# A planned attention-and-recurrence kernel: a shift of rank for each part of the work, and measured lengths for bunches of small matmuls

## The chip, the cores and the metric

The kernel runs on one core of a Trainium2 chip, in float32 throughout. The core has five engines with a queue of instructions each: TensorE (PE) for matmuls, VectorE (DVE), ScalarE (ACT), GpSimd (POOL), and SyncE (SP), which issues the transfers (DMAs). Each engine works through its own queue in order; engines wait for each other by semaphores. The metric is device time in microseconds, lower is better. The kernel before takes 1836.63 us (median of three runs, 1832.29 to 1839.57).

## The reference, cut to what matters

There are 32 batches. Each has two matrices of 128 x 512. A cross attention comes first, then one block of a recurrent layer with 32 heads of size 16 over a sequence of 128 steps.

```python
# attention, for each batch: x_c = x, x_s = ctx
Mn = Wn @ inorm(x_c) + bn;  Mm = Wm @ inorm(x_s) + bm
A  = softmax(Mn.T @ Mm, axis=-1)                   # 512 x 512
x  = Wo @ ((Wl @ x_s + bl) @ A.T) + bo + x_c
# recurrent block, 128 steps, 512 channels
xa = ln(x); sx = shift(xa) - xa                    # shift: the step before
xxx = tanh((xa + sx * maa_x) @ maa_w1)             # five mixes
xk, xw, xv, xr, xg = (xa + sx * (maa_j + xxx_j @ maa_w2_j) for j in "kwvrg")
w = exp(-exp(time_decay + tanh(xw @ td_w1) @ td_w2))
r, k, v, g = xr @ Wr.T, xk @ Wk.T, xv @ Wv.T, silu(xg @ Wg.T)
for t in range(128):                               # for each head: state s, 16 x 16
    a = outer(k[t], v[t]);  out[t] = r[t] @ (u * a + s);  s = a + w[t][:, None] * s
x1 = x + (groupnorm(out) * g) @ Wo.T
xc = ln(x1); xk2, xr2 = two more mixes of xc with its shift
return x1 + sigmoid(xr2 @ Wfr.T) * (square(relu(xk2 @ Wfk.T)) @ Wfv.T)
```

## The kernel before, in words

The 32 batches form eight groups of four (`G = 4`, `NG = 8`), so a tile holds 128 channels by 4 x 128 steps: 128 x 512. `layer0(b)` is the attention of one batch: four matmuls of scores (128 x 512 each), a maximum on DVE, an exponential on ACT, the division on DVE, sixteen transposes on PE with copies on ACT, and four matmuls with the values. `layer1(g)` is the recurrent block of a group. Its parts follow each other: the front (normalisation, shift, low-rank matmuls), the mixes (DVE, then POOL adds), gates, two halves of the recurrence (`c = 0` and `c = 2`, two tiles of channels each), the head (group norm, `Wo`), and `feed_forward` (norm, squares, rows, and the store of the result).

The recurrence has no loop over steps. Scores between steps are made level by level, for blocks of 1, 2, 4, 8, 16 and 32 steps: after each level DVE multiplies r and k by decays (`twice`), ACT spreads r over two tiles (`wide`), and a *bunch* of 64 small matmuls (32 rows each) makes the scores, which DVE copies under a mask (`level`), or ACT plainly for the last level, into `at`. When all levels are done, the scaled k is transposed (8 transposes in a bunch), copied by ACT, and three kinds of bunches follow: the state in mid-sequence (32 matmuls, `ps`), the outputs from the state (64, `po`), and twice 64 matmuls that add `at` times v.

The kernel's code does not fix the order of instructions. `Program.record` keeps every operation, and `Program.run` (line 225 on) asks `schedule` for an order and emits it; so all instructions bear line L234. `schedule` is a planner: it estimates each operation's length (`cost`; a bunch's is written by hand in `K.bunch(ns)`), and `order_of` walks through time and takes, among the operations that can start soonest on an engine, the one with the lowest rank. The rank is the operation's place in the written order, less a small share of the length of the chain behind it. In sixteen rounds the planner lowers the ranks of what came before PE's longest gaps, and keeps the best order by its own reckoning. It also decides which buffer each tensor gets: 8 banks of PSUM, 44 work tiles (`t`), and four places for weights of 1 MB (`wring`). The attention of the next group's batches is written in among the parts of the present group (`ahead`), so that PE has other work during the recurrence. The last two groups overlap in another way: the feed-forward of group 6 runs within group 7 (`later`, `place`).

SP issues all large transfers in the order that the planner gives. Four weights pass through each of the four `wring` places in turn; `Wg`, `Wk` and `Wr` for a group are loaded while the group before ends, when its `Wo`, `Wfk`, `Wfr` and `Wfv` leave their places. The stores of the result (`out_dram`, four per group) go through the same queue, after a POOL addition each.

Of the kernel before, what the change touches and what calls it, by code (L numbers as in the profile page):

```python
# [23 lines left out]
G = 4  # L24
NG = B // G
# [34 lines left out]
LAG = 130  # L60
SWITCH = 95
ROUNDS, TRACE, BLAME = 16, 20000, 0.001
REACH, PULL = 200, 0.003
WORDS, REFILL = 280, 3200
TABLE = {AF.Exp: ("exp",), AF.Tanh: ("exp", "sigmoid"), AF.Sigmoid: ("sigmoid",), AF.Sqrt: ("sqrt",)}
# [230 lines left out]
    return ns, ns  # L296


def schedule(ops):


    for op in ops:
        for b in op.before:
            b.after.append(op)


    chain = [0.0] * len(ops)
    for op in reversed(ops):
        i = op.index
        chain[i] = op.ns + max(  # L310
            [chain[a.index] + LAG for a in op.after if a.index < i + REACH], default=0.0
        )
        op.rank = i - PULL * chain[i]
    best = None
    for turn in range(ROUNDS):
        order = order_of(ops)
        end = max(op.end for op in ops)
        if best is None or end < best[0]:
            best = end, order, [(t, t.slot) for op in ops for t in op.first], [op.rank for op in ops]
            since = 0  # L320
        else:
            since += 1
        if since == 4:

            for op, rank in zip(ops, best[3]):
                op.rank = rank
            since = 0
        free = 0.0
        for op in order:
            if op.engine != "PE":  # L330
                continue
            gap, free = op.start - free, op.end
            if gap < 200:
                continue
            late = op
            while late and late.end > op.start - TRACE:
                late.rank -= BLAME * min(gap, 3000) * (1 + turn % 4)
                late = max(late.before, key=lambda b: b.end, default=None)
    for t, slot in best[2]:
        t.slot = slot  # L340
    return best[1]
# [203 lines left out]
def xattn_then_rwkv(ctx: ExitStack, tc: tile.TileContext, a: dict, out: bass.AP):  # L545
# [74 lines left out]
        return vec[:, i, c : c + 1]  # L620

    def constants():
        K.stage = ("constants",)

        def load(t, src):
            K.held = begun[0]
            K.sync.dma_start(t, src)

        load(vec, a["vec"])
        rows = wt([2 * B, E])  # L630
        for r in range(2):
            load(rows[r * B : (r + 1) * B, :], a["ctx_2048"][:, r, :])
        load(w1, a["maa_w1"].rearrange("(c p) m -> p c m", p=P))
        load(w2a, a["maa_w2"][0:P, :])
        for c in range(NC):
            load(w2b[c * DM : (c + 1) * DM, :], a["maa_w2"][P : P + DM, c * P : (c + 1) * P])
        load(td1, a["td_w1"].rearrange("(c p) m -> p c m", p=P))
        for i in range(2):
            load(td2[i * DD : (i + 1) * DD, :], a["td_w2"])
        load(wv, a["WvT"].rearrange("(c p) o -> p c o", p=P))  # L640


        pt = bank()
        for c in range(NC):
            K.tensor.transpose(
                pt[:, c * 2 * B : (c + 1) * 2 * B], rows[:, c * P : (c + 1) * P],
                ident[0 : 2 * B, 0 : 2 * B],
            )
        K.vector.tensor_copy(st.rearrange("p c r b -> p (c r b)"), pt[:, 0 : NC * 2 * B])

        def block_ones(t, pattern, first, step, width):

            K.gpsimd.memset(t, 1.0)
            K.gpsimd.affine_select(
                out=t, in_=t, compare_op=ALU.is_ge, fill=0.0, base=first,
                pattern=pattern, channel_multiplier=step,
            )
            K.gpsimd.affine_select(
                out=t, in_=t, compare_op=ALU.is_ge, fill=0.0, base=width - 1 - first,
                pattern=[[-s, n] for s, n in pattern], channel_multiplier=-step,  # L660
            )


        for n in (DM, DD):
            part = st_(n)
            K.vector.tensor_reduce(part, ident.rearrange("p (i m) -> p m i", m=n), AX.X, ALU.add)
            K.vector.tensor_copy(
                fold[n].rearrange("p (i m) -> p i m", m=n),
                part.unsqueeze(1).to_broadcast([P, P // n, n]),
            )  # L670

        block_ones(heads, [[-S, DM]], 0, 1, S)

        K.vector.tensor_copy(sum_bc, heads[:, 0:H8].unsqueeze(2).to_broadcast([P, H8, S]))

        K.vector.tensor_reduce(
            par, heads[:, 0:H8].rearrange("p (q x) -> p x q", x=2), AX.X, ALU.add
        )

        K.vector.tensor_scalar(heads, heads, 1.0 / S, None, ALU.mult)  # L680


        for l in level:
            flt = st_(C // 2)
            for n in range(2):
                block_ones(flt[n * C : (n + 1) * C, :], [[-2 * l, C // 2 // l], [0, l]], 0, 1, l)
            K.vector.tensor_copy(level[l], flt)

        for c in range(NC):
            block_ones(heads_t[c * DM : c * DM + H8, :], [[1, P]], 0, -S, S)  # L690


        wvh = wv.rearrange("p c (h j) -> p (c h) j", j=S)
        wvm = wt([P, NC * NH])
        K.vector.tensor_reduce(wvm, wvh, AX.X, ALU.add)
        K.vector.tensor_scalar(wvm, wvm, 1.0 / S, None, ALU.mult)
        K.vector.tensor_tensor(
            wvh, wvh, wvm.unsqueeze(2).to_broadcast([P, NC * NH, S]), ALU.subtract
        )
# [17 lines left out]


    def layer0(b):
        K.stage = ("first", b)  # L720
        x_c, x_s = wt(), wt()
        K.held = begun.get(b - 2)
        K.sync.dma_start(x_c, a["x"][b])
# [114 lines left out]
    def recurrence(c, ex, xk, xr, xv, wk, wr, s0m):  # L838
# [5 lines left out]
        for i in range(2):  # L844
            K.scalar.copy(r[i], proj(wr, xr, c + i))
            K.scalar.copy(k[i], proj(wk, xk, c + i))
            K.scalar.copy(v[i], proj(wv, xv, c + i))

# [48 lines left out]
        for i in range(2):  # L900
# [14 lines left out]
            for s in range(2):  # L915
                K.vector.tensor_tensor(right, right, t2.view(s, (4, nb), (2, 2)), ALU.add)

        for l in LEVELS:


# [6 lines left out]
                    AF.Identity, scale=par[:, x : x + 1],  # L927
                )
            pa = [bank() for _ in range(Q4)]
            with K.bunch(2 * 843):  # L930
                for i in range(2):
                    for b in range(G):
                        for n in range(2):
                            for q in range(Q4):
                                rows_q = slice(q * DM, (q + 1) * DM)
                                at_ = i * N + b * L + n * C
                                K.tensor.matmul(
                                    pa[q][n * C : (n + 1) * C, (i * G + b) * C : (i * G + b + 1) * C],
                                    rk[rows_q].view(2 * N + at_, (1, C)),
                                    r2[rows_q, (i * G + b) * 2 + n],  # L940
                                    start=True, stop=True,
                                )
# [31 lines left out]
            kt.append(wt([C, N]))  # L974
            K.scalar.copy(kt[i], pk[i][0:C, :])
        ps = bank()
        with K.bunch(2 * 385):
            for i in range(2):
                for b in range(G):
                    for q in range(Q4):  # L980
                        at_ = i * VP + (b * Q4 + q) * 2 * DM
                        K.tensor.matmul(
                            ps[q * DM : (q + 1) * DM, (i * G + b) * DM : (i * G + b + 1) * DM],
                            kt[i][:, b * P + q * DM : b * P + (q + 1) * DM],
                            vp[0:C].view(at_, (DM + S, 2), (1, S)),
                            start=True, stop=True,
                        )
        s1 = wt([P, 2 * G, 2 * S])
        for x in range(2):
# [3 lines left out]
                ALU.mult, ALU.add,  # L993
            )


        po = [bank() for _ in range(2)]
        with K.bunch(2 * 1020):
            for i in range(2):
                for b in range(G):  # L1000
                    for n in range(2):
# [7 lines left out]
                                start=(i == 0 and b == 0), stop=False, skip_group_check=True,  # L1009
                            )  # L1010
        for i in range(2):
            with K.bunch(2 * 760):
                for b in range(G):
                    for x in range(2):
                        for n in range(2):
# [18 lines left out]
    def layer1(g, xs):  # L1034
# [14 lines left out]
                    if p == i:  # L1049
                        next(later[0])  # L1050

        K.stage = ("front", g)
        s0 = wt([P, G, NC, S])
        for i in range(G):
            K.held = begun[g * G + 1]
# [46 lines left out]
        low_g = wt()  # L1102
        K.scalar.activation(low_g, pl, AF.Tanh)


        xm = {n: [] for n in "kwvrg"}
        pg = [bank() for _ in range(NC)]
# [41 lines left out]
        dlow = wt()  # L1149
        K.scalar.activation(dlow, pd, AF.Tanh)  # L1150

        gates = []
        for c in range(NC):
            pg = proj(wg, xm["g"], c)
# [4 lines left out]

        o = []  # L1160
        for c in range(0, NC, 2):
            K.stage = ("recurrence", g, c)
            if g == NG - 1 and c == 2:
                last_ws[:] = [weight(n, holds) for n in ("Wfk", "Wfr")]
            holds = K.ops[-1]
            place(c // 2)
            K.stage = ("recurrence", g, c)
            ex = decays(c, dlow)
            K.stage = ("recurrence", g, c)
            if c == 2:  # L1170
                third = K.ops[-1]
            ahead(c)
            o += recurrence(c, ex, xm["k"], xm["r"], xm["v"], wk, wr, s0m)
            ahead(c + 1)
        K.stage = ("back", g)
        wo = weight("Wo", third)
        if g == NG - 1:
            last_ws.append(weight("Wfv", third))
# [1 line left out]
            ws = [weight(n, third) for n in ("Wfk", "Wfr", "Wfv")]  # L1180

        place(2)
        K.stage = ("back", g)

        pvar = bank()
        sq = []
# [44 lines left out]

    def feed_forward(g, xs, ws):

        K.stage = ("back", g)
        xc, sx2 = norm_shift(xs, "ln2_w", "ln2_b", 0, g)
        xk2, xr2 = [], []
        for c in range(NC):
# [6 lines left out]
            )  # L1244
            xr2.append(sx2[c])
        yield
        K.stage = ("back", g)
        kk = []
        for eo in range(NC):
            pk = proj(ws[0], xk2, eo)  # L1250
# [2 lines left out]
            K.vector.tensor_tensor(t, t, pk, ALU.mult)  # L1253
            kk.append(t)
        yield
        K.stage = ("back", g)
        wfr, wfv = ws[1:]
        for i in range(G):
            sl = slice(i * L, (i + 1) * L)
# [64 lines left out]
```

## Time and profile before

| what | us |
|---|---|
| median of three runs | 1836.63 |
| the profiled execution's own time | 1835.13 |
| its span, first to last instruction | 1833.4 |
| PE busy | 1775.9 (97%) |
| DVE busy | 1170.1 (64%) |
| ACT busy | 704.2 (38%) |
| POOL busy | 310.0 (17%) |
| one matmul pass of 128 x 512, start to start (a matmul takes two) | 0.43 |
| a bunch of level scores, shortest | 1.52 |
| 1 MB of weights, issue to landing | 5.0 to 6.8 |

In a row of the timeline stand the start, the length of the merged instructions, the engine, line, operation, tiles (written<-read), shape, how many records, and in brackets the idle time of the engine ahead of it with what ended it. A float32 matmul leaves two records, a transpose one; so a bunch of 64 matmuls has 128. PEclk is the share of PE's clock that was granted. "issue" as a reason means that the profile shows nothing that the engine waited for.

### The profile page before, as it was taken

Reading aid. Unit: us, or ns where it says so; the run is one execution under the profiler, and the core shown is the slowest. Engines: PE = TensorE matmul, PEld = TensorE weight load, DVE = VectorE, ACT = ScalarE, POOL = GpSimd, SP = SyncE. Lnnn points to the kernel's source line nnn. Section 1 sums busy time; section 2 is a strip of 40 time slices with the busy share of each in tenths; the row PEclk is TensorE's granted clock in tenths of the full one; section 3 lists DMA queues with packets and bytes.
Section 4 is the critical chain, followed back from the end, with each engine's and each line's share of the span. In section 5 each row is a group of like instructions: output and inputs, shape, how many; then the busy total and the mean of one; then the engine's idle time right before and its main releaser. Section 6 shows DMA issues by size and latency. Waiting matters only on the chain. (4 is left out here: it accounts for less than half of the span.)

```text
span 1833.4 us, 45471 instructions
## 1 busy us (share of the span) xinstructions
PE 1775.9 (97%) x20232; PEld 885.6 (48%) x20232; DVE 1170.1 (64%) x2301; ACT 704.2 (38%) x1230; POOL 310.0 (17%) x329
## 2 busy tenths in 40 slices
PE   8999999999999999999999999999999999999998
PEld 4445543455434554345543455434554345545543
DVE  9748783398634886448764487645876466756652
ACT  5334531445313553235532354323543254324421
POOL 2320006000060001600016000160000600410011
PEclk9999999999999999999999999999999999899999
DMA  6002112020121101221011110112101121002000
GB/s 208 23 23 63 26 54 73 23 71 19 58 69 46 52 14 58 69 70 29 14 63 65 69 30 14 63 63 70 30 13 64 41 60 49 3 24 71 4 18 29
DMA packets 61939, 87.22 MB, mean 48 GB/s; under 512 B 20336, under 2 KB 21488, under 8 KB 61744
## 3 DMA queue, kind: packets, MB, share of 16 engines
q1 hardware_dynamic: 61024, 84.06, 14.2%
q8 instruction: 158, 2.59, 0.6%
q14 instruction: 37, 0.30, 0.1%
q10 hardware_dynamic: 720, 0.26, 0.1%
HBM read 75.93 MB, written 8.39 MB: 46 GB/s over the span
## 5 line engine op out<-in xcount | busy, mean ns | idle before, releaser
L234 PE MATMUL bank<-t,wring 128*128 128x512 f32 x1024 | 473.4, 599 | 3.4 <-DVE t L234 3.3
L234 PE MATMUL bank<-wring,t 128*128 128x512 f32 x768 | 342.5, 597 | 0.0
L234 DVE TENSOR_TENSOR t<-bank,t 128x512 f32<-128x512 f32 (+1 forms) x256 | 143.8, 585 | 265.5 <-PE bank L234 182.0
L234 PEld LDWEIGHTS bank<-t,wring 128*128 128x128 f32 x1024 | 184.4, 190 | 238.4 <-issue 209.0
L234 POOL TENSOR_TENSOR t<-t,t 128x512 f32<-128x512 f32 x192 | 239.9, 1287 | 312.0 <-DVE t L234 311.3
L234 POOL TENSOR_TENSOR small<-small,neg_half 128x1 f32<-128x1 f32 (+1 forms) x96 | 62.5, 663 | 1206.1 <-DVE small L234 1196.9
L234 PE MATMUL bank<-t,t 128*128 128x512 f32 x512 | 255.1, 609 | 0.2 <-ACT t L234 0.2
L234 PEld LDWEIGHTS bank<-wring,t 128*128 128x128 f32 x768 | 143.9, 191 | 189.9 <-issue 179.8
L234 ACT COPY t<-bank 128x512 f32<-128x512 f32 (+1 forms) x240 | 132.2, 588 | 228.7 <-PE bank L234 222.0
L234 ACT ACTIVATE t<-bank 128x512 f32<-128x512 f32 x120 | 71.5, 597 | 367.7 <-PE bank L234 283.1
L234 DVE SCALAR_TENSOR_TENSOR t<-bank,vec,t 128x512 f32<-128x512 f32 x192 | 134.3, 745 | 60.1 <-PE bank L234 49.9
L234 PEld LDWEIGHTS bank<-ident,t 128*128 128x128 f32 x900 | 106.9, 140 | 95.5 <-issue 61.7
L234 PE MATMUL bank<-ident,t 128*128 128x128 f32 x900 | 141.2, 277 | 3.5 <-ACT at L234 2.4
L234 ACT ACTIVATE wide<-rk,par 128x512 f32<-128x512 f32 x128 | 85.4, 715 | 127.2 <-DVE rk L234 127.0
L234 PE MATMUL bank<-t,wv 128*128 128x512 f32 x256 | 123.8, 598 | 0.2
L234 PEld LDWEIGHTS bank<-wide,rk 32*64 32x64 f32 x8192 | 96.9, 131 | 55.9 <-issue 27.1
L234 PEld LDWEIGHTS bank<-t,t 128*128 128x128 f32 x512 | 85.4, 189 | 79.0 <-issue 52.4
L234 DVE COPY_PREDICATED at<-level,bank 128x512 f32<-128x512 int32 x192 | 123.1, 706 | 0.0
L234 ACT ACTIVATE t<-bank,small 128x512 f32<-128x512 f32 x128 | 87.6, 688 | 89.6 <-DVE small L234 88.1
L234 PE MATMUL bank<-wide,rk 32*64 32x64 f32 x8192 | 108.0, 233 | 7.9 <-issue 5.2
L234 DVE TENSOR_REDUCE small<-bank 128x1 f32<-128x512 f32 x128 | 85.4, 685 | 38.2 <-PE bank L234 37.9
L234 DVE TENSOR_SCALAR t<-t,small,small 128x512 f32<-128x512 f32 x128 | 67.4, 546 | 39.9 <-POOL small L234 36.8
(98 smaller groups left out, 1815.7 us busy)
## 6 DMA issues: line engine op xcount, KB each, us to landing
t<-in_ctx_dram SPq DMA_DIRECT2D x32, 256.0 KB, 3.0
t<-in_x_dram SPq DMA_DIRECT2D x32, 256.0 KB, 3.0
wring<-in_WgT_dram SPq DMA_DIRECT2D x8, 1024.0 KB, 5.5
wring<-in_WkT_dram SPq DMA_DIRECT2D x8, 1024.0 KB, 5.1
wring<-in_WrT_dram SPq DMA_DIRECT2D x8, 1024.0 KB, 5.3
wring<-in_WoT_dram SPq DMA_DIRECT2D x8, 1024.0 KB, 5.5
out_dram<-t SPq DMA_DIRECT2D x32, 256.0 KB, 2.0
wring<-in_WfkT_dram SPq DMA_DIRECT2D x7, 1024.0 KB, 5.0
```

What stands on the lines that cost most here:

```text
L234: f(*[real(x) for x in args], **{k: real(x) for k, x in kw.items()})
```

## The change

Each recorded operation already carried the name of its part (`K.stage`). The change gives the stages finer names and all of them the same form (kind, group or batch, half), adds a table of shifts in rank by stage, and adds an operation's shift to its rank; a key with "+" holds for the last groups in addition (the last four batches for "first", the last two groups for others). The shifts were found by random trials of the planner. Besides, four lengths of bunches are set to values measured on the chip. Nothing else is changed: no operation, no buffer count.

```diff
+SHIFTS = {
+    "first0": -306, "first0+": -95, "first1": 2, "first1+": -122, "first2": -40,
+    "first2+": -7, "first3": 24, "first3+": 203, "front": 7, "front+": 157, "gates": -67,
+    "gates+": -1, "head": -121, "head+": 51, "levels0": -68, "levels0+": -71, "levels2": 20,
+    "levels2+": -152, "mixes": 81, "mixes+": -41, "norm": 78, "norm+": -310,
+    "outputs0": -277, "outputs0+": 238, "outputs2": -235, "outputs2+": -661,
+    "recurrence0": -14, "recurrence0+": -48, "recurrence2+": -68, "rows": 85, "rows+": 306,
+    "squares": -88, "squares+": 77, "values0": -56, "values0+": -63, "values2": 33,
+    "values2+": 81,
+}
...
+def shift(op):
+    kind, of, sub = op.stage
+    last = of >= (NG - 1) * G if kind == "first" else of >= NG - 2
+    return SHIFTS.get(kind + sub, 0) + (SHIFTS.get(kind + sub + "+", 0) if last else 0)
...
-        op.rank = i - PULL * chain[i]
+        op.rank = i - PULL * chain[i] + shift(op)
...
-            with K.bunch(2 * 843):        # level scores
+            with K.bunch(1522):
...
-        with K.bunch(2 * 385):            # state in mid-sequence
+        with K.bunch(686):
...
-        with K.bunch(2 * 1020):           # outputs from the state
+        with K.bunch(1920):
...
-            with K.bunch(2 * 760):        # at times v
+            with K.bunch(1412):
```

The new stage names: "first" with the batch's place in its group, "recurrence" split into "recurrence", "values", "levels" and "outputs" (each with its half, 0 or 2), "front" split into "front", "mixes" and "gates", and "back" into "head", "norm", "squares" and "rows".

More of the change, by code (lines that the diff above doesn't have):

```diff
@@ L622, in constants @@
     def constants():
-        K.stage = ("constants",)
+        K.stage = ("constants", 0, "")
         def load(t, src):
@@ L719, in layer0 @@
     def layer0(b):
-        K.stage = ("first", b)
+        K.stage = ("first", b, str(b % G))
         x_c, x_s = wt(), wt()
@@ L847, in recurrence @@
             K.scalar.copy(v[i], proj(wv, xv, c + i))
+        K.stage = ("values", K.stage[1], K.stage[2])
         VP = G * Q4 * 2 * DM
@@ L916, in recurrence @@
                 K.vector.tensor_tensor(right, right, t2.view(s, (4, nb), (2, 2)), ALU.add)
+        K.stage = ("levels", K.stage[1], K.stage[2])
         for l in LEVELS:
@@ L994, in recurrence @@
             )
+        K.stage = ("outputs", K.stage[1], K.stage[2])
         po = [bank() for _ in range(2)]
-        with K.bunch(2 * 1020):
+        with K.bunch(1920):
             for i in range(2):
@@ L1050, in place @@
                         next(later[0])
-        K.stage = ("front", g)
+        K.stage = ("front", g, "")
         s0 = wt([P, G, NC, S])
@@ L1103, in layer1 @@
         K.scalar.activation(low_g, pl, AF.Tanh)
+        K.stage = ("mixes", g, "")
         xm = {n: [] for n in "kwvrg"}
@@ L1150, in layer1 @@
         K.scalar.activation(dlow, pd, AF.Tanh)
+        K.stage = ("gates", g, "")
         gates = []
@@ L1161, in layer1 @@
         for c in range(0, NC, 2):
-            K.stage = ("recurrence", g, c)
+            K.stage = ("recurrence", g, str(c))
             if g == NG - 1 and c == 2:
@@ L1166, in layer1 @@
             place(c // 2)
-            K.stage = ("recurrence", g, c)
+            K.stage = ("recurrence", g, str(c))
             ex = decays(c, dlow)
-            K.stage = ("recurrence", g, c)
+            K.stage = ("recurrence", g, str(c))
             if c == 2:
@@ L1174, in layer1 @@
             ahead(c + 1)
-        K.stage = ("back", g)
+        K.stage = ("head", g, "")
         wo = weight("Wo", third)
@@ L1182, in layer1 @@
         place(2)
-        K.stage = ("back", g)
+        K.stage = ("head", g, "")
         pvar = bank()
@@ L1232, in feed_forward @@
     def feed_forward(g, xs, ws):
-        K.stage = ("back", g)
+        K.stage = ("norm", g, "")
         xc, sx2 = norm_shift(xs, "ln2_w", "ln2_b", 0, g)
@@ L1246, in feed_forward @@
         yield
-        K.stage = ("back", g)
+        K.stage = ("squares", g, "")
         kk = []
@@ L1255, in feed_forward @@
         yield
-        K.stage = ("back", g)
+        K.stage = ("rows", g, "")
         wfr, wfv = ws[1:]
```

## The prediction

> **What bounds the kernel now.** I read the page first:
>
> ```profile
> span 1833.4 us, 45471 instructions
> PE 1775.9 (97%) x20232; PEld 885.6 (48%) x20232; DVE 1170.1 (64%) x2301; ACT 704.2 (38%) x1230; POOL 310.0 (17%) x329
> PEclk9999999999999999999999999999999999899999
> ```
>
> TensorE (PE) is the bound: it is idle for 1833.4 - 1775.9 = 57.5 us. Of these, 6.3 pass before its first matmul (the chain of waits names the DMA of WoT) and 5.1 after its last, which ends at 1828.3. So 46.1 us are left to an order, and besides them what is hidden inside "busy": bunches of small matmuls that run long, and time at half clock. Next, busy time by stretch (the columns after the stretch: its length, then PE, weight loads, DVE, ACT, POOL, PE clock, DMA):
>
> ```profile
> 604.00:690.00 86.00, 81.47 (x1909) 48.72 (x1897) 70.58 (x142) 45.89 (x88) 3.75 (x6) 1.00 0.09 23
> 690.00:829.00 139.00, 138.38 (x632) 60.53 (x635) 73.59 (x144) 42.31 (x66) 33.54 (x30) 1.00 0.19 65
> 829.00:915.00 86.00, 80.75 (x1909) 48.42 (x1901) 70.79 (x142) 45.91 (x88) 3.75 (x6) 0.98 0.09 23
> 915.00:1057.00 142.00, 141.39 (x648) 61.87 (x649) 73.67 (x144) 42.30 (x66) 33.55 (x30) 1.00 0.18 63
> 454.48:457.89 3.41, 3.41 (x4) 1.34 (x5) 3.41 (x6) 0.69 (x1) 0.00 (x0) 0.50 0.00 0
> 1580.88:1591.12 10.24, 9.07 (x176) 5.09 (x165) 9.83 (x14) 3.39 (x6) 9.39 (x7) 0.50 0.01 2
> 680.00:683.41 3.41, 2.46 (x5) 0.97 (x6) 3.41 (x6) 1.13 (x2) 0.00 (x0) 1.00 0.00 0
> ```
>
> A group takes about 226 us, and its idle sits in one part: 4.5 and 5.3 us in the 86 us from mid-recurrence to the head, 0.6 in the 140 us between. The five such parts of groups 1 to 5 sum to 24.3 us, 0 to 240 us holds 9.5 after the first matmul, and 1546 to 1612 us 4.4. The timeline of PE in group 3, and two places of group 2 that recur in each group, say what ends the waits:
>
> ```profile
> 839.07 1.59 PE L234 MATMUL bank<-wide,rk 32*64 32x64 f32 x128
> 842.13 1.06 PE L234 MATMUL bank<-ident,rk 128*64 128x128 f32 x8 [1.47 <-DVE rk L234]
> 844.62 0.76 PE L234 MATMUL bank<-vp,t 64*32 64x32 f32 x64 [0.57 <-ACT t L234]
> ...
> 858.07 1.12 PE L234 MATMUL bank<-wide,rk 32*64 32x64 f32 x80
> 859.89 0.77 PE L234 MATMUL bank<-wide,rk 32*64 32x64 f32 x48 [0.70 <-issue]
> 860.59 1.12 PE L234 MATMUL bank<-t,t 128*128 128x512 f32 x2
> ```
> ```profile
> 680.95 1.12 PE L234 MATMUL bank<-t,WnT 128*128 128x512 f32 x2 [1.11 <-DVE t L234]
> 706.75 2.81 PE L234 MATMUL bank<-t,wring 128*128 128x512 f32 x6 [0.58 <-DVE t L234]
> ```
>
> PE has run out of other ready work there; its DVE or ACT partner then sets the end.
>
> **The change part by part.** It adds and removes no instruction: matmuls, ACT table loads (46) and 194 transfers are the same. All of it is the order, read from the built programs. I lay PE's instructions out at their undisturbed traced durations and ask, for each wait, how much PE work stands between the instruction that starts a chain and the one that needs its result.
>
> *Bunch lengths.* 1686 becomes 1522 ns for a bunch of level scores, others likewise. The chip's bunch costs what it did (the one at 1568.54 is followed at 1570.06): 0 us by itself. Only the planner's idea of what covers a chain gets truer.
>
> *Groups 1 to 5, the 86 us part.* (1) Between the last level bunch and the transposes of k stood nothing; the need is 842.13 - 839.07 - 1.52 = 1.54 us. Now two projection matmuls of 0.86 us and two changes of tile shape stand there, 1.81 us: saves 1.54. (2) Transposes to the state bunch: need 1.62, cover 0.95, now 3.52: saves 0.63. (3) The next half's first level bunch came 1.6 us after the previous bunch and took 860.59 - 858.07 = 2.52 instead of 1.52; now 11.7 us lie between: saves 1.00. (4) State bunch to output bunch in the second half: 0.85 us apart, with stretches of 0.28 and 0.66; now 2.0. Bunches 1.9 apart still stretch by 0 to 0.77, so half: 0.5. (5) Transposes of the softmax at 880 us waiting for DVE: 0.38. (6) The bank held by the head's product (680.95): 1.27 with the restart. (7) 706.75: 0.75. For 5 to 7 no chain of the new order lacks over 0.06 us of cover. Sum 6.07 per group. Against it: this ignores queues on DVE, busy 70.6 of 86 us. In the order before, chains alone explain about 3.4 of the 4.6 us of waits, so queues added 1.2; I leave 1.2 in: 4.87 x 5 = 24.4 us. Ends: 12 (half comes back) and 30 (none).
>
> At (3) the Trainium skill speaks against me: "Runtime: NRT & Kernel Launch", Instruction fetch mechanics, says that code is fetched in 16 KiB blocks of 256 instructions and that crossing into the next is mostly hidden. A bunch has 128 matmul and 128 weight-load records, one block. By the rule, spacing is worth 0 and 3 and 4 fall away (-7.5 us); the row shows 1.00 us at one bunch. I go by the row.
>
> *Group 0.* The first phase of batch 4 moves ahead of group 0's front (places 102 to 169 of PE's 2740 planned operations, before 136 to 189). POOL's twenty adds of 1.29 us for the mixes are then later: about 4 us more wait near 90 us. Later the order has the covers of (1) and (2), where waits of 1.8, 0.9, 0.7 and three of 0.5 stood, and stretches that sum to 2.8: about 8. Net 4, ends 0 and 8.
>
> *From group 6 to 7 (1546 to 1612 us).* Four level bunches stand close; the new order leaves 0.53 us between the third and fourth and 0 before the transposes: 3.2 + 1.6 us uncovered, against 4.4 idle before. POOL's adds for the last mixes lack about 9 us of cover, where they lacked 14. Gain 2, ends -4 and +6. Group 7's output bunches go from 0.95 to 1.8 us apart: gain 1, ends 0 and 2.
>
> *Half clock.* At 454 and 908 us the clock halves for 3.41 us after wait (6): 2 x 1.7 us. "TensorE: Matmul & The Clock Gate", What's actually happening, asks for an idle window of about 3.4 us; the row has 1.11 us of idle, and at 680 us the same wait left the clock at 1.00. By the rule closing (6) brings 0 here, by the row up to 3.4: I take 2. The rule also warns that the 3.2 us hole at group 6 to 7 may halve the clock again; so of the 10.24 + 6.83 us at half clock there (8.5 us) I count nothing as won.
>
> *Shapes and DMA.* Changes of tile shape fall from 461 to 456, 0.09 us each: 0.5. SP issues in order, and WrT stands behind three output stores; before, it was issued at 750.75 and used at 757.46, 6.7 us for a load of about 5.3:
>
> ```profile
> 750.75 0.39 SPq L234 DMA_DIRECT2D wring<-in_WrT_dram  x1
> ```
>
> Now the PE work between the slot's release and the use is 0.8 us shorter: 5.9 us, still enough; I charge 0.5, up to 3.
>
> Sum: 24.4 + 4 + 2 + 1 + 2 + 0.5 - 0.5 = 33.4 us. The profiled execution took 1835.1 (1833.4 span and 1.7 around it): 1801.7. The median of the runs is 1836.6, 1.5 above; I give **1803 us**.
>
> **The rivals.** *Queues take half back.* DVE is busy 82% of the 86 us part; the chains get cover but arrive behind others. For it: 1.2 us per group already. Against: the idle is at few places. Half of 33: 1819 us.
>
> *No change.* The trials fitted the planner, which knows nothing of half clock and guesses the fetch of code; PE then waits at new places. Against: the uncovered places of 3.4 us per group are gone in the order itself. 1836 us, within 0.5%, which is about what a measurement of this kernel can tell.
>
> *Slower: POOL holds up WrT.* The third store waits for POOL's third output add. One mix add stood ahead of that add in POOL's row of outputs and mixes; now eight do (10 us). By durations the store is ready 2.4 us before WrT's slot (3.3 before), and WrT has 0.6 us to spare. If the add comes over 3.0 us later than that, PE stops at the projection, each further us costing 1 us in five groups. From 3.0 + 33.4 / 5 = 9.7 us on the kernel is slower; at 13 us it ends at 1853. Against: POOL has 4.2 of 16.9 us free there.
>
> **How the numbers follow.** Likeliest 62%, own range 1790 to 1815: the ends of the parts, not all at once. Queues 22%, 1815 to 1827. No change 9%. Slower 7%. The bound of 0.5% lies at 1827.4, so faster is 0.84, same 0.09, slower 0.07. The range of 8 in 10 runs from 1788 to 1828.
>
> **What would show it.** In the 86 us parts PE idle falls from about 5 to 1 to 2 us; the 1.47 wait for rk and the 1.11 before WnT are gone; the first level bunch of the second half takes 1.5 us; no half clock near 454 and 908 us; near 1500 to 1600 us waits and half clock stay. I am wrong if PE's waits for DVE in groups 1 to 5 keep their sum, if a wait for WrT appears, or if PE's busy time grows by what its idle loses.

## The result, and the profile after

The changed kernel takes 1808.97 us (median; 1808.35 to 1811.91) beside 1834.46 (1829.71 to 1839.57) for the kernel before on the same chip: a ratio of 0.9864, 95% interval 0.9833 to 0.9895, or 25.5 us less. Beside the other experiments it gave 1808.25 and 0.9872 (0.9857 to 0.9886). Forecast were 1803 us, with 1788 to 1828 as the range: the sign and the range were right. The time is 6 us above the forecast; of the forecast gain of 33.4 us, 8 are missing (the kernel before, measured again, took 2 us less than in the forecast). How the 25.5 us came about is not how the forecast summed them.

The head of the page after, as the prediction showed it of before:

```profile
span 1807.2 us, 45445 instructions
PE 1761.2 (97%) x20232; PEld 889.7 (49%) x20232; DVE 1170.0 (65%) x2301; ACT 706.0 (39%) x1230; POOL 310.0 (17%) x329
```

PE's idle time is 1807.2 - 1761.2 = 46.0 us (57.5 before), and its busy time is 14.7 us less for the same 20232 matmuls: part of the gain was hidden in "busy". What PE waited for, first the kernel before, then the changed one (in total, times, longest, all in us):

```profile
PE bank L234 <- issue: 13.4, 28, 1.4
PE bank L234 <- DVE t L234: 12.2, 16, 1.1
PE bank L234 <- DVE rk L234: 7.3, 5, 1.5
PE bank L234 <- ACT t L234: 4.9, 8, 1.6
```
```profile
PE bank L244 <- issue: 17.4, 20, 2.4
PE bank L244 <- DVE t L244: 6.6, 7, 1.8
PE bank L244 <- ACT t L244: 4.9, 10, 1.8
PE bank L244 <- DVE rk L244: 1.4, 1, 1.4
```

The waits for DVE have shrunk, as forecast: those for rk from five to one. But "issue", time in which PE waited for nothing that the profile shows, has grown from 13.4 to 17.4 us, and its longest from 1.4 to 2.4. Busy time by stretch (columns: the stretch, its length, PE, weight loads, DVE, ACT, POOL, PE clock, DMA share, GB/s):

```profile
458.00:595.00 137.00, 136.71 (x892) 62.76 (x891) 82.04 (x160) 43.61 (x68) 34.84 (x32) 1.00 0.14 47
595.00:681.00 86.00, 82.49 (x1642) 48.01 (x1641) 62.03 (x129) 44.97 (x86) 2.89 (x4) 1.00 0.18 53
815.00:901.00 86.00, 84.58 (x1716) 49.54 (x1705) 64.27 (x135) 47.22 (x89) 2.89 (x4) 1.00 0.18 53
384.16:387.57 3.41, 3.41 (x36) 1.98 (x36) 1.09 (x1) 1.33 (x2) 0.00 (x0) 0.50 0.87 204
97.44:104.26 6.82, 6.82 (x11) 2.84 (x10) 3.77 (x6) 0.00 (x0) 6.82 (x7) 0.50 0.01 2
```

The five 86 us parts now hold 1.4 to 4.2 us of idle, 3.0, 3.5, 1.4, 2.8 and 4.2 in groups 1 to 5, where the prediction said 1 to 2. The half clock of 454 and 908 us is gone; there is a new one at 97 us, 6.8 us long, and in this execution one at 384.

To see more than idle I took each piece of PE work (a planned operation) from its start to the next one's start, against the undisturbed time of the same kind of work. What is over is excess, and I sorted it: waits for other engines; half clock; excess of the bunches of 32 or more small matmuls that is no such wait ("code"); and the rest. Each number is one execution's. In us, before then after:

| part of the kernel | waits | half clock | code | rest |
|---|---|---|---|---|
| group 0 | 6.4, 3.4 | 0, 3.4 | 3.7, 3.5 | 10.4, 9.2 |
| groups 1 to 5 | 20.0, 3.2 | 3.4, 1.7 | 13.0, 16.7 | 25.8, 19.1 |
| to the passage from 6 to 7 | 0.9, 1.0 | 0, 0 | 1.3, 0.2 | 3.6, 2.6 |
| passage | 4.3, 6.7 | 8.2, 4.4 | 0.9, 1.0 | 2.0, 2.2 |
| end | 0.4, 2.5 | 0, 0 | 5.6, 1.9 | 2.4, 3.2 |
| all | 32.0, 16.7 | 11.6, 9.5 | 24.5, 23.4 | 44.3, 36.2 |

In groups 1 to 5 the waits fell by 16.8 us. The "code" excess, of which the prediction took 7.5 us away, rose by 3.7. Here is where it sits: PE's timeline in group 2 of the changed kernel, from the last level bunch of the first half to its second output bunch, then the first level bunch of the second half, and SP's queue.

```profile
592.36 1.59 PE L244 MATMUL bank<-wide,rk 32*64 32x64 f32 x128
593.88 1.98 PE L244 MATMUL bank<-t,wring 128*128 128x512 f32 x4
595.70 1.05 PE L244 MATMUL bank<-ident,rk 128*64 128x128 f32 x8
...
600.11 0.76 PE L244 MATMUL bank<-vp,t 64*32 64x32 f32 x64
600.80 1.13 PE L244 MATMUL bank<-t,wring 128*128 128x512 f32 x2
601.76 1.02 PE L244 MATMUL bank<-t,wv 128*128 128x512 f32 x2
602.72 1.87 PE L244 MATMUL bank<-rk,t 32*32 32x64 f32 x119
606.46 0.35 PE L244 MATMUL bank<-rk,t 32*32 32x64 f32 x9 [1.87 <-issue]
...
608.65 1.37 PE L244 MATMUL bank<-at,vp 64*32 64x64 f32 x115
611.01 0.34 PE L244 MATMUL bank<-at,vp 64*32 64x64 f32 x13 [0.99 <-issue]
...
626.91 1.59 PE L244 MATMUL bank<-wide,rk 32*64 32x64 f32 x128
```
```profile
599.36 0.37 SPq L244 DMA_DIRECT2D wring<-in_WfrT_dram  x1
601.96 0.37 SPq L244 DMA_DIRECT2D wring<-in_WfvT_dram  x1
```

The transposes of k (595.70) follow two projection matmuls and wait for nothing; that is step (1) as forecast. The projections of the second half, PE's cover, now run to 601.93 us. They are the last readers of two wring places, and WfvT is issued into one of these 0.03 us later. So the cover itself puts two loads of 1 MB (landing at 604.6 and 608.6 us) on the output bunches, whose first then stops for 1.87 us in mid-bunch with no engine to wait for. Before, the same loads had landed 22 us ahead of the first output bunch, which ran through:

```profile
591.32 0.37 SPq L234 DMA_DIRECT2D wring<-in_WfrT_dram  x1
593.03 0.37 SPq L234 DMA_DIRECT2D wring<-in_WfvT_dram  x1
```
```profile
622.11 2.27 PE L234 MATMUL bank<-rk,t 32*32 32x64 f32 x128
```

### The profile page after: what moved, and what is told of

Same layout as the page of the kernel before. It is cut to its first block, busy times and chain, and to the rows that moved or that the text cites. A ratio compares the mean times of both kernels' runs of the same rounds, so it can differ in the third digit from the quotient of the medians.

```text
span 1807.2 us, 45445 instructions
## 1 busy us (share of the span) xinstructions
PE 1761.2 (97%) x20232; PEld 889.7 (49%) x20232; DVE 1170.0 (65%) x2301; ACT 706.0 (39%) x1230; POOL 310.0 (17%) x329
## 3 DMA queue, kind: packets, MB, share of 16 engines
q1 hardware_dynamic: 61024, 84.06, 14.7%
q8 instruction: 158, 2.59, 0.6%
## 5 line engine op out<-in xcount | busy, mean ns | idle before, releaser
L244 PE MATMUL bank<-t,t 128*128 128x512 f32 x512 | 251.1, 607 | 2.2 <-ACT t L244 2.2
L244 PE MATMUL bank<-ident,t 128*128 128x128 f32 x900 | 130.2, 276 | 3.8 <-ACT t L244 2.7
L244 DVE SCALAR_TENSOR_TENSOR t<-t,vec,t 128x512 f32<-128x512 f32 x128 | 90.9, 755 | 0.1
```

The costliest lines, as they stand in the source:

```text
L244: f(*[real(x) for x in args], **{k: real(x) for k, x in kw.items()})
```

## The experiments

Two theories on the gain and two on what is missing of it. *Cover*: PE work between the ends of a chain replaces waits one for one. *Given back*: a wait gives the code time to arrive, so that closing it only moves the stop. *Loads*: the two 1 MB loads hold up the fetch of PE's code. *Spacing*: a bunch stops because it follows another too closely, whatever is being loaded. Each kernel is compared with runs of the kernel before taken beside it.

| kernel | median, us | before beside it | ratio (95% interval) |
|---|---|---|---|
| changed kernel | 1808.25 | 1831.1 | 0.9872 (0.9857 to 0.9886) |
| ... without the ten loads | 1796.11 | 1831.1 | 0.9809 (0.9795 to 0.9824) |
| ... loads held back behind the outputs | 1796.28 | 1831.1 | 0.9811 (0.9795 to 0.9826) |
| ... cover (1) undone | 1819.45 | 1831.1 | 0.9932 (0.9918 to 0.9947) |
| shifts with old lengths | 1827.28 | 1832.88 | 0.9975 (0.9965 to 0.9986) |
| new lengths without shifts | 1852.57 | 1832.88 | 1.012 (1.0099 to 1.0141) |
| before without the ten loads | 1831.74 | 1832.88 | 0.9997 (0.9986 to 1.0008) |
| loads held back, batch 4 unshifted | 1793.24 | 1832.88 | 0.9794 (0.9774 to 0.9814) |
| changed, loads under level bunches | 1801.61 | 1831.6 | 0.9833 (0.9815 to 0.9851) |
| before, loads under output bunches | 1864.4 | 1831.6 | 1.0171 (1.0152 to 1.019) |
| loads held back, no shifts for the last groups | 1810.79 | 1831.6 | 0.988 (0.986 to 0.9899) |

### The changed kernel again

> The changed kernel again, as the measure for the three others of this call: 1809 us, with the bunches of matmuls that begin the outputs of the first half stretched by 1.2 to 3.0 us in each of groups 1 to 5, as in its first profile.

1808.25 us; the code excess of groups 1 to 5 is 18.4 us, and the same bunches stop: in groups 1 to 5 the first-half output bunches are over by 1.82 + 1.74, 1.86 + 1.48, 1.25, 2.15 and 2.64 us.

### Without the loads

```diff
         for op in order:
+            if op.stage[0] == "head" and 1 <= op.stage[1] <= 5 and op.calls[0][1] == "dma_start":
+                if op.calls[0][2][1].tensor.name in ("in_WfrT_dram", "in_WfvT_dram"):
+                    continue
```

> The changed kernel without the ten loads of WfrT and WfvT in groups 1 to 5, so the feed-forward of those groups computes with other weights; PE's instructions and their order stay. Theory 'loads': the two 1 MB loads in flight hold up the fetch of PE's code. Then the stretches at the output bunches of the first half (3.04, 2.10 + 1.21, 1.24, 2.16 and 2.66 us in groups 1 to 5) fall to under 0.5 each, and the time falls by 9 to 12 us, to 1797 to 1800. Theory 'spacing': a bunch stretches because the one before it ended too short a time ago, whatever is being loaded. Then the stretches stay within 0.3 us each and the time is 1809, give or take 2.

1796.11 us, 12.1 less than the changed kernel. The code excess of groups 1 to 5 falls from 18.4 to 5.2 us (-13.2); their waits stay at 3.1 and the rest at 19.3 (19.1). The output bunches of group 2, same order, same distances, run through:

```profile
598.59 1.99 PE L247 MATMUL bank<-rk,t 32*32 32x64 f32 x128
602.42 1.59 PE L247 MATMUL bank<-at,vp 64*32 64x64 f32 x128
```

"Loads" holds for these stops. "Spacing" alone can't be their cause: PE's order is the same, instruction for instruction, and nothing but the loads is left out. About 1 us a group is left of the code excess. One stop was to go under 0.5 us and did not: an output bunch of group 1 is still over by 0.71.

### The loads held back

```diff
         for op in order:
-            for attr, method, args, kw in op.calls:
...
+            kind, g, _ = op.stage
+            if kind == "head" and 1 <= g <= 5 and op.calls[0][1] == "dma_start" and ends:
+                if g in ends and op.calls[0][2][1].tensor.name in ("in_WfrT_dram", "in_WfvT_dram"):
+                    held.setdefault(g, []).append(op)
+                    continue
+            if ends.get(g) is op:
+                self.emit(op)
+                acc = real(op.calls[0][2][0])[:, 0, 0:1]
+                for load in held.get(g, ()):
+                    w = real(load.calls[0][2][0])[:, 0, 0:1]
+                    self.nc.gpsimd.tensor_tensor(w, acc, acc, ALU.add)
+                    self.emit(load)
```

Here `ends[g]` is the last DVE operation of the first half's outputs.

> The changed kernel with the loads of WfrT and WfvT of groups 1 to 5 held back until the accumulation of the first half's outputs (an add of one element on POOL per load, which reads that result, gates each), so that they run in the 11 us without a bunch that follow, over 70 us ahead of their use. Nothing else moves. 'Loads': the stretches at the first half's output bunches go, 1797 to 1801 us. 'Spacing': they stay, 1809. A third outcome, loads harm whatever bunch they meet: the stretches move to the first level bunches of the second half (at 627 us in group 2), and under half of the gain is left, 1803 to 1808.

1796.28 us: the same gain, with nothing left out of the work. Contrary to the expectation's words something else does move: the x and ctx loads behind these two in SP's queue come after them as well, at 610.5 us. Timeline and queue of group 2:

```profile
598.72 1.99 PE L267 MATMUL bank<-rk,t 32*32 32x64 f32 x128
...
602.55 1.49 PE L267 MATMUL bank<-at,vp 64*32 64x64 f32 x128
```
```profile
609.52 0.37 SPq L267 DMA_DIRECT2D wring<-in_WfrT_dram  x1
610.00 0.45 SPq L267 DMA_DIRECT2D wring<-in_WfvT_dram  x1
```

The three 86 us parts that I cut out of this trace (370, 590 and 806 us on) hold 0.4, 0.6 and 0.8 us of idle. The gain is not due to the x and ctx loads: in the run without the ten loads they went out at 597.5 to 601 us, beside the output bunches, and these did not stop.

What is late can be read in the trace's DMA records. The page's queue "q8 instruction" moved 2.59 MB in 158 packets, 16.4 KB each. The Trainium skill, "Runtime: NRT & Kernel Launch", section "Instruction fetch mechanics", says that a sequencer fetches its code in 16 KiB blocks through a DMA queue of its own; the packets agree in size, and PE's 20232 matmul and 20232 weight-load records are 158 blocks of 256 and a rest of 16, as many blocks as there are packets. DMA traffic in two windows, first the changed kernel from 602 to 606 us, then the one with held-back loads from 597 to 600:

```profile
q1 hardware_dynamic: 766, 1.54, 102.9%
q8 instruction: 1, 0.02, 1.6%
```
```profile
DMA  0000000900000000000000000000000000000000
q8 instruction: 1, 0.02, 2.4%
```

With the loads in flight the 16 engines are full, and the block's packet starts 3.81 us after the first half's state bunch. With the loads held back it is the only traffic and starts 1.45 us after the same bunch; over groups 1 to 5 the packet comes 2.6 us later in the mean with the loads than without. The packet itself takes 1.05 us in the one and 1.13 in the other: it starts late, it doesn't run long. In the changed kernel it ends at 604.98 us, and PE goes on at 606.46.

That PE waits for code in these stops can be read off as well. Number all records of PE (matmuls, weight loads, its sequencer's) from 0 in the order of time. In the thirteen traces of this case, past the first 20 us, PE stops 117 times for 0.5 us or more with "issue" as the reason; 116 of these stops end at a record whose number leaves 193 or 194 when divided by 256, each 1.2 to 1.6 us after a packet of this queue has ended. So the stops sit at the borders of blocks of 256 instructions. In the changed kernel's trace 117 of the 158 packets start with the DMA engines idle since the last border, and half of them start 0.84 to 1.16 us behind it. In the place above PE passes the border at 600.62 us and the packet starts 3.31 us later; with the loads held back it passes at 596.62 and the packet starts 0.95 us later. That the packet stands in line behind the loads' packets in between is inferred; when it was asked for isn't recorded.

### Cover (1) undone

```diff
-        order = schedule(self.ops)
+        order = uncovered(schedule(self.ops))
...
+        if mine and op.calls[0][1] == "transpose":
...
+            out += [op] + kept
...
+        if op.engine == "PE" and seen.get(g) == 4 and not mine:
+            kept.append(op)
+            continue
```

The 4 is the last level bunch: a half has four, for blocks of 4, 8, 16 and 32 steps. Blocks of 1 and 2 steps are worked on DVE, without a bunch.

> The changed kernel with one piece of its order undone: in the first half of groups 1 to 5 the two projection matmuls between the last level bunch and the transposes of k come behind the transposes instead. Theory 'cover': PE again waits for the scaling of k, about 1.5 us in each of five groups, and the time grows by 6 to 8 us, to 1815 to 1817. Rival 'given back': code is fetched during that wait, so the stretched output bunch some 6 us later shrinks by as much, and the time grows by less than 2 us.

1819.45 us, 11.2 more than the changed kernel, where "cover" expected 6 to 8. PE's waits for rk in total, and group 2:

```profile
PE bank L244 <- DVE rk L244: 9.8, 6, 1.7
```
```profile
593.36 1.59 PE L244 MATMUL bank<-wide,rk 32*64 32x64 f32 x128
596.69 1.06 PE L244 MATMUL bank<-ident,rk 128*64 128x128 f32 x8 [1.74 <-DVE rk L244]
...
605.43 1.87 PE L244 MATMUL bank<-rk,t 32*32 32x64 f32 x119
609.05 0.35 PE L244 MATMUL bank<-rk,t 32*32 32x64 f32 x9 [1.75 <-issue]
```

The wait comes back (9.8 - 1.5 = 8.3 us in five places, 1.66 each), and the stop of the output bunch 9 us later is nearly as long as with the cover (1.75 against 1.87). "Given back" falls. That leaves 2.9 us. The trace shows windows of half clock in groups 2, 4 and 5 that the changed kernel's two traces do not have, two of them:

```profile
609.98:613.39 3.41, 3.41 (x72) 1.39 (x74) 0.52 (x1) 1.33 (x2) 0.00 (x0) 0.50 0.67 127
1043.47:1046.88 3.41, 3.41 (x10) 1.85 (x8) 0.10 (x1) 2.46 (x5) 0.00 (x0) 0.50 0.00 0
```

With the others at 1060.5 and 1285.8 us they come to 13.6 us at half clock, up to 6.8 us of time. Over all executions the mean granted clock is 0.9910 here (six) and 0.9925 in the changed kernel (four). If all of that is lost time, it is 0.0015 x 1819 = 2.7 us, an estimate that would account for the remainder; with so few executions it is no more than likely.

### Shifts or lengths alone

The first kernel takes the old lengths back (2 * 843, 2 * 385, 2 * 1020, 2 * 760) and keeps `SHIFTS`; the second is the kernel before with these four edits:

```diff
-            with K.bunch(2 * 843):
+            with K.bunch(1522):
...
-        with K.bunch(2 * 385):
+        with K.bunch(686):
...
-        with K.bunch(2 * 1020):
+        with K.bunch(1920):
...
-            with K.bunch(2 * 760):
+            with K.bunch(1412):
```

> The shifts of rank with the old bunch lengths. The planner's order then has four projection matmuls ahead of the transposes of k in the first half of groups 1 to 5 (two in the changed kernel, none before). If the shifts bring the gain: waits of PE for other engines in groups 1 to 5 near 3 us in sum (20 before) and a time within 6 us of the changed kernel, 1803 to 1815. If the lengths are needed for it: 1820 or more.

> The measured bunch lengths without the shifts. The order still has nothing between the last level bunch and the transposes of k in the first half of groups 1 to 5, so the wait of 1.5 us for k's scaling stays there. If the shifts bring the gain: no gain, within 5 us of the kernel before, 1826 to 1836. If truer lengths alone let the planner cover the chains: 1820 or less.

1827.28 us: the waits in groups 1 to 5 did fall to 3.1 us, but not the time. The profiled execution, 1820.4 us of span, has the rest at 25.3 us there (19.1 in the changed kernel), and 5.1 us of half clock in the end, where the changed kernel has none. The medians differ by 19.0 us, the profiled spans by 12.3 to 13.2. Most of this is half clock that the trace doesn't show: the profiled execution is the fastest of the 22, 5.1 us below their median, at a clock of 0.993 where the 22 have 0.9908 in the mean, by an estimate 0.0022 x 1827 = 4 us. Where the rest of what the waits gave was lost is open. And 1852.57 us for the lengths alone, 20 us slower than before, worse than either expectation: with truer lengths and no shifts the order still has nothing ahead of the transposes of the first half, and the waits of groups 1 to 5 rise to 30.7 us, with 8.0 of half clock. The two parts are worth -0.3% and +1.2% alone and -1.3% together. The shifts were found by trials of a planner with the new lengths; a list of ranks found for one set of costs gives another order with the other.

### The kernel before without the loads

The edit is that of "Without the loads", with the stage name that the kernel before has there (`back`).

> The kernel before without its loads of WfrT and WfvT in groups 1 to 5 (those groups' feed-forward computes with other weights), as the control to the same edit of the changed kernel, which took 12 us off. There the loads ran at 591 to 602 us in group 2, ahead of the output bunches. If loads harm through the place that the new order gives them: 0 to 2 us faster than before, with code stretches still near 13 us in groups 1 to 5. If loads harm wherever they lie: 8 us faster or more.

1831.74 us, ratio 0.9997 (0.9986 to 1.0008): no gain where the changed kernel gained 12.1. The code excess of groups 1 to 5 is 10.1 us in its trace (13.0 with the loads). So the cost isn't the loads as such; it came with the place that the new order gave them.

### The loads under other bunches

Two more places: in the changed kernel under the second half's level bunches (gated by the first DVE operation of the second half's values behind its first level bunch), and in the kernel before under the output bunches (gated by the DVE operation that reads the state bunch).

> The changed kernel with its loads of WfrT and WfvT of groups 1 to 5 held back further: a one-element add on POOL per load, behind an addition on DVE that follows the first level bunch of the second half, lets them go at about 630 us in group 2, so that they run under the second and third level bunches (632 and 638 us there, each some 5 us after the bunch before it). If loads harm any bunch of small matmuls that is fetched beside them: these level bunches take 2.5 to 4 us instead of 1.38 and half or more of the 12 us comes back, 1802 to 1808. If they harm only bunches that follow another at 1 to 2 us, as the output bunches do: 1796 to 1799, with level bunches at 1.38.

> The kernel before with its loads of WfrT and WfvT of groups 1 to 5 held back until the state of the first half is accumulated (a one-element add on POOL each), so that they lie under the output bunches of the first half, as the new order has them. If the loads' place is the cost: those bunches, which took 2.06, 1.27 and 1.66 us in group 2, take 2 to 4 us, and the time grows by 6 to 12 us, to 1839 to 1845. If it took the new order as well: within 3 us of before.

1801.61 us lies between the two outcomes, near the first: 5.3 of the 12 us come back (medians measured at different times), with a code excess of 11.2 us in groups 1 to 5 (4.6 with the loads behind the outputs). A level bunch some 5 us behind the one before it is hit as well, less often, but hard in group 5:

```profile
1284.52 1.54 PE L271 MATMUL bank<-wide,rk 32*64 32x64 f32 x123
1289.85 0.48 PE L271 MATMUL bank<-wide,rk 32*64 32x64 f32 x5 [3.79 <-issue]
```

In group 2 the second level bunch took its usual 1.38 us from first to last matmul and the third 2.07. The kernel before with the loads on its outputs takes 1864.4 us, 32.8 more, where 6 to 12 were expected. Group 2, PE then DVE:

```profile
634.25 0.90 PE L261 MATMUL bank<-at,vp 64*32 64x64 f32 x69
638.17 1.13 PE L261 MATMUL bank<-at,vp 64*32 64x64 f32 x59 [3.02 <-issue]
640.92 3.71 PE L261 MATMUL bank<-t,sum_bc 128*128 128x512 f32 x4 [1.61 <-DVE t L261]
```
```profile
639.17 0.42 DVE L261 TENSOR_REDUCE small<-t 128x16 f32<-128x256 f32 x1 [6.06 <-DMA t<-in_ctx_dram]
```

The stop is 3.02 us. A side effect adds to it: a ctx load behind the two in SP's queue comes late, DVE stands 6.06 us for it at the head of its queue, PE then 1.61 for DVE, and from 637.6 us the clock is at half for 6.8 us. Waits of groups 1 to 5 rise to 33.5 us and half clock to 20.9 (20.0 and 3.4 before). As a measure of time this run is spoilt by the ctx load. What the loads do to the code can be read apart from it: the excess of the first half's output bunches rises from 2.2 to 11.4 us in groups 1 to 5, with one stop of about 3 us in each of groups 1 to 4. That is "loads' place", without the new order.

### Batch 4 unshifted, and the shifts of the last groups

On top of the held-back loads. The first leaves the first phase of batch 4 without a shift, the second drops what holds only for the last groups:

```diff
+    if kind == "first" and of == G:
+        return 0
     return SHIFTS.get(kind + sub, 0) + (SHIFTS.get(kind + sub + "+", 0) if last else 0)
```
```diff
-    return SHIFTS.get(kind + sub, 0) + (SHIFTS.get(kind + sub + "+", 0) if last else 0)
+    return SHIFTS.get(kind + sub, 0)
```

> The changed kernel with its loads of WfrT and WfvT held back as in the run before, and with no shift for the first phase of batch 4, which then stays where the kernel before had it, behind the start of group 0's front. If that phase delays POOL's adds for the mixes of group 0, as the prediction said, the waits and the half clock near 93 to 104 us (3.4 + 3.4 us in excess there) mostly go: 3 to 6 us faster than with the loads held back alone, 1790 to 1794. If the hole is the chain of the front itself: 1796 within 2 us.

> The changed kernel with WfrT and WfvT held back behind the outputs (1796 us) and without the further shifts that hold for the last groups alone; the order of groups 1 to 5 stays as it is. By the prediction's sum the change gained 2 us at the passage from group 6 to 7 and 1 in group 7: 1797 to 1801. If the last groups' shifts are worth nothing or cost: 1796 or less. If the planner's list needs them far more: 1805 or more.

1793.24 us, about 3 less than with the loads held back alone; the intervals of the two ratios overlap, so the difference isn't sure. It is the lowest time of all. The mean clock of four executions each, 0.9962 beside 0.9948, would be 2.5 of the 3 us. In its trace group 0 loses 6.3 us of excess (waits 3.9 to 2.2, half clock 3.4 to none, code 3.1 to 2.2), while the new plan happens to lose 3.5 at the passage from group 6 to 7. The hole near 93 us, first in the changed kernel, then without that shift:

```profile
96.28 4.04 PE L244 MATMUL bank<-t,w2a 32*128 32x512 f32 x8 [1.77 <-DVE t L244]
```
```profile
94.14 2.84 PE L267 MATMUL bank<-t,wring 128*128 128x512 f32 x6 [0.93 <-DVE t L267]
...
98.97 1.08 PE L267 MATMUL bank<-t,td 128*64 128x512 f32 x4 [0.91 <-issue]
```

In the changed kernel DVE comes to the operation that PE waits for at 95.48 us, and without a pause: up to then, from 90.91 us on, it works on others that stand ahead (`TENSOR_SCALAR`, `RECIPROCAL`, `TENSOR_REDUCE`). POOL's next add starts at 96.37 us and has itself waited 1.62 us for DVE.

1810.79 us without the last groups' shifts, 14.5 more than with them: the third outcome. The order of groups 1 to 5 is the same. By the excess 16.8 us are lost behind the passage and 5.3 ahead of it, and 6.4 are won in group 0, where the new plan differs too (97 us is passed at full clock: six or seven projection matmuls stand ahead of each bunch there, in place of the two ahead of the one that waited 1.77 us for DVE). So the plain shifts spoil the end, and most of what the further ones do there is to repair that; beside the order of before, passage and end gained only about 2 us. And the hole near 93 us goes away in a plan with batch 4 shifted as well: the place of that phase is one way to it, not the only one.

## Why the prediction was right, and which step failed

- *Bunch lengths, 0 us by themselves.* Right for the chip's bunches; but the prediction did not say that the shifts are worth little without them.
- *(1), (2), (5), (6), (7), less 1.2 for queues.* 3.37 us per group, 16.9 in five, were forecast; the waits of groups 1 to 5 fell by 16.8. Two small ones remain per group, 0.44 and 0.23 us, both for ACT. For (1) the undone cover shows the price: 1.66 us per place against the 1.54 read off.
- *(3) and (4), spacing, 7.5 us.* Both came true at their own bunches, and the step that failed stands next to them: the sum has no term for the first half's output bunches. The code excess of groups 1 to 5 by kind of bunch, in us:

| bunches | before | changed | changed, without the loads | before, loads under outputs |
|---|---|---|---|---|
| first level bunch of the second half (3) | 4.8 | 0.0 | 0.0 | 2.0 |
| outputs from the state, second half (4) | 2.4 | 0.0 | 0.0 | 1.6 |
| three output bunches, first half | 2.2 | 13.2 | 2.5 | 11.4 |
| all others | 3.7 | 3.5 | 2.7 | 1.7 |

(3) and (4) brought 7.2 us, and the first half's outputs took 11.0. What the prediction left out is that the cover of (1) and (2) is the last reader of two wring places. WfrT went out 28.2 us ahead of the state bunch of group 2 before (591.3 and 619.5 us) and goes out 0.7 us ahead of it now (599.4 and 600.1), and so both load under the output bunches: 12.1 us by the run without them, 2.4 per group. Under "Shapes and DMA" the prediction looked at loads for one thing only, whether WrT would come too late to be used. It never asked what code would be fetched beside them.

- *The skill's rule against (3) and (4).* That crossing into the next block is mostly hidden holds better in the changed order with quiet DMA (about 1 us per group left) than in the order before (2.6), and not at all beside two 1 MB loads (3.3 to 3.7 us per group). Going by the row was right for (3) and (4); neither the row nor the rule, as I used them, had the loads in it.
- *Group 0, net 4.* About 1. The loss near 90 us was priced at 4 us and came as 1.8 of wait and 3.4 of half clock. Its place was right; the engine was not, since PE waits there for DVE, which is busy with other work, not for POOL's adds, and the cover that is missing can come from gate projections as well as from another place of batch 4's phase.
- *Passage and group 7, 3 us.* By the table 15.4 to 14.3 us at the passage and 8.4 to 7.6 in the end: about 2.
- *Half clock, 2 us.* 11.6 to 9.5 us of excess in the two profiled executions, though 6.8 us at half clock have turned up at 97 us. Over more executions the mean clock is 0.9929 before (65) and 0.9933 after (8), an estimated 13.0 and 12.2 us: a gain of 2 is not shown.
- *WrT.* 0.5 was charged; no wait for WrT appears among PE's waits. So the slower rival did not happen. The rival that queues take half back saw a loss of the right kind, part of the gain given back, in the wrong place: no queue on DVE, but PE's code.
- *Not foreseen.* The rest fell by 8.1 us, 6.7 of it in groups 1 to 5. It is made of short stops, most near 0.1 us. In groups 1 to 5 the passes of 128 x 512 that take 0.5 to 0.8 us from start to start in place of 0.43 became fewer, 290 to 258, which is 3.7 us; what the others are I can't say. This luck hid two thirds of the loads' cost: without it the time would be near 1817 us, still within the range of 1788 to 1828, but not within the likeliest outcome's own range of 1790 to 1815.

In one sum: 33.4 forecast, less 12 for the loads, less 3 for group 0, less 1 for passage and end, plus 8 of the rest: 25.4, beside 26.2 by the two profiled executions (1835.1 to 1808.9). The sum is put together after the fact from single executions; shown by runs of their own are the loads' 12 us and the price of cover (1).

## What to carry to other kernels

Work that is moved to cover a wait holds its buffers longer and later; ask which load takes that buffer next, and which code runs while it lands. Where bunches of many small instructions and bulk loads can be kept apart, a gate of one element on an idle engine does it: here 12 us of 1808, for a load that is needed over 70 us later. And ranks found by search belong to the costs they were searched with: half of such a change is not half of its gain.

## What the runs showed that was not expected

- Beside two 1 MB loads (388 GB/s from 602 to 606 us) PE's next 16.4 KB of code start 2.6 us later in the mean, and PE stops for 1 to 3.8 us in mid-bunch, up to twice per group, at the border of a block of 256 instructions. 256 KB and 32 KB loads at the same place did not do this.
- A stop of PE brings half clock at one time and not at another. In each trace all windows of half clock begin on one grid of 3.41 us. Counted over the thirteen traces: of the grid's windows at full clock, all 19 in which PE was idle for 2.0 us or more were followed by half clock, 35 of the 125 with 1.0 to 2.0 us, and 3 of the 2869 with less. So chance has a part: the stop of 2.39 us in group 1 of the changed kernel lay whole in one window, and half clock followed at 384.16 us; that of 1.87 us in group 2 lay across two, and none followed. With cover (1) undone, four windows of groups 2, 4 and 5 had 1.75 to 2.48 us of idle, and half clock followed each. What decides between 1.0 and 2.0 us I could not tell.
